# Four graph layers in one kernel: Horner's rule in the last layer, scores beside the context, weights' sums one at a time

## The chip, the cores and the metric

The kernel runs on one core of a Trainium2 chip. The time is the device time of one execution in microseconds (us); all times in this text are microseconds unless marked ns. The core has a matrix engine (TensorE, PE in the rows, with its weight loads as PEld), three engines for elementwise work (VectorE or DVE, ScalarE or ACT, GpSimd or POOL) and a queue that issues most DMAs (SyncE or SP). Everything is float32.

## What is computed

128 graphs of 64 nodes with 512 features pass through four layers. Each layer normalises, applies relu and adds its result to x. Cut to what matters:

```python
h = maximum(layernorm(x), 0)                  # before every layer
# layer 0
agg = adj @ (k * mask); w = D**-0.5 * mask * sum(q * agg, -1)
x += softmax(w over the nodes)[:, None] * (h @ Wv)
# layer 1: q, k, v with biases
W = adj * exp(q @ k.T); x += (W / W.sum(-1)) @ v
# layer 2: 8 heads of 64, q, k, v with biases
P = softmax((q @ k.T) * D_h**-0.5 * (adj + adj)); x += concat(P @ v) @ Wo + bo
# layer 3
e = leaky_relu(sj[None, :] + si[:, None] + ab)
alpha = A * exp(e); Tm = alpha / (alpha.sum(-1) + 1e-12)
x += relu(h @ Wk[0] + Tm @ h @ Wk[1] + Tm @ Tm @ h @ Wk[2] + bk.sum(0))
```

## The kernel before

**Blocks.** The 8192 tokens are 32 blocks of 256 (four graphs), each two tiles of 128 tokens (two graphs). Layers 0 and 1 run for two blocks at a time (layer 0 on b and b+1, layer 1 on b and b+1), then layer 2 for all blocks, then layer 3. x goes through DRAM between layers 1, 2 and 3.

**Products.** A product of a block (256 x 512) with a weight (512 x 512) is done with seven half-size products (the Strassen-Winograd form). `sums` (L203) makes four sums of the activations on POOL (S1, S2, S4, S3; L215 to L218), `formed` (L83) four sums of a weight's quarters (T1, T2, T4, T3). A `Product` (L227) has four accumulators in two PSUM banks, `ab` and `dc`, from a pool of four. `first` issues products 1 and 6 and reads both banks' first state off (`keep_ab`: p1 on ACT, u2 on DVE); `second` issues 5 and 4 and reads p5 off; `late` issues 2, 7 and 3 on top, and `store` adds the pieces up on ACT, DVE and POOL. Product 6 needs S2, product 5 needs S1. `side_by_side` (L339) runs two products with the same activations: first and second of each, then late and store of each, and calls other work (`between`) at three places: after the first's `first`, before the first's `late`, before the second's `late`. A matmul in float32 is two passes of TensorE, so a product is 28 passes of 128x256, or 56 of 128x128 where the output has the features in partitions (`feature_major`, L243).

**Layer 0** multiplies with M, the product of the key and query weights, made once (`folded`, L416: `pf` in the rows, 32 passes), with both weights transposed first (`transpose_weight`, L403: `tw`). At the start the first block's values are multiplied ahead of M (L938 to L942). **Layer 1** has an M of its own, made by `setup1` (L439) inside the first call of `layer1`. Its end takes, per block, the row sums (`den`, L575) and `neighbour_sums` (L377): the matmuls with the attention matrix as weights, 64 rows by 64 columns each, for the four graphs at once in the four quarters of the array.

**Layer 2** per block b: `layer2_scores` (the 64x64 score products into two slots of the PSUM pool `ps_sc`, then softmax), the products for q and k of block b+1, `layer2_turned` (transposes of the softmax), the first half of the values of b+1, `layer2_context` (64x64 products of v and softmax into `ps_sc`, copied out by two ACT copies), the late half of the values, and the output product. Before it, `setup2` (L592) multiplies the values' bias with Wo (`pb`, L608) and adds it to the output bias; that row is added to x on POOL (L991).

**Layer 3** per block: `layer3_norm` (L775: norm, two weighted row sums of h per tile on DVE as `hu` L787, and a diagonal matrix of one of them), then `layer3_in` (L802): a matmul with ones spreads the diagonal (`graph_sums`, L389), e and alpha are made, divided by their row sums and put into a block-diagonal matrix `bd`; two matmuls with `bd` give the transposed transition and its square (`pn`, L833); 16 matmuls multiply h with both (`pz`, L849), ACT copies the result as z, and `sums` is made for h and both parts of z. `layer3_out` (L863) then adds all three products into one pair of accumulators: for each of the seven products, three matmul pairs, one for each Wk. DVE and POOL add the bias, relu and x.

**Order.** Each engine runs its queue in order. The order in the queues comes from the builder: an earlier statement ranks higher, but where an engine would stand idle by the builder's own estimate, ready work of a later statement is put ahead (the trace shows layer 2's loads of adj issued at 21.0). A tile's buffer is reused when its last reader is done.

Of the kernel before, what the change touches and what calls it, by code (L numbers as in the profile page):

```python
# [8 lines left out]
FP = mybir.dt.float32  # L9
AF = mybir.ActivationFunctionType  # L10
ALU = mybir.AluOpType
# [14 lines left out]
def kernel(ctx: ExitStack, tc: tile.TileContext, a: dict, out: bass.AP):  # L26
# [55 lines left out]

    def formed(w, engine):  # L83
        engine.tensor_tensor(w[:, T1], w[:, T3], w[:, B11], ALU.subtract)
        engine.tensor_tensor(w[:, T2], w[:, B22], w[:, T1], ALU.subtract)
        engine.tensor_tensor(w[:, T4], w[:, B21], w[:, T2], ALU.subtract)
        engine.tensor_tensor(w[:, T3], w[:, B22], w[:, T3], ALU.subtract)
# [41 lines left out]
    w0v = fetched("L0_Wv", 1, nc.scalar)  # L129
# [18 lines left out]


    n_bd = 2  # L150
    bds = []
    for i in range(n_bd):
        e = const.tile([P, TT, P], FP, tag=f"bd{i}", name=f"bd{i}")
        nc.gpsimd.memset(e, 0.0)
        bds.append(e)
    turn = [0]

    def next_bd():
        turn[0] += 1
        return bds[turn[0] % n_bd]  # L160
# [61 lines left out]
    class Product:  # L222
# [40 lines left out]
        def first(self, ops, w):  # L263
            self.early(ops, w, (1, 6))
            self.keep_ab()

        def second(self, ops, w, bias=None):
            self.early(ops, w, (5, 4))
            self.keep_dc(bias)
# [69 lines left out]
    def side_by_side(*parts, between=()):  # L339
# [5 lines left out]
        for ops, w, bias, store, name in parts:  # L345
            p = Product(name, bias is not None)
            p.first(ops, w)
            if not made:
                for act in next(between, ()):
                    act()  # L350
            p.second(ops, w, bias)
            made.append(p)
# [77 lines left out]
    def setup0():  # L430
        transpose_weight(f0[1], "k0")
# [7 lines left out]
    def setup1():  # L439


        w1v = fetched("L1_Wv", 3, nc.sync)
        qT, kT = (factor(a[f"L1_W{c}"], c, 1, nc.sync) for c in "qk")
# [28 lines left out]
        return m, u, c, d, w1v, [weight(f"L2_W{c}", 4 + i, nc.sync) for i, c in enumerate("qk")]  # L472


    made1 = []

    def layer0_values(b: int, hT):
        ops = sums(hT, f"0_{b}")
        gv = big.tile([P, 2, TT, D], FP, tag="qk", name=f"gv_{b}")
        return ops, gv, (ops, w0v, None, lambda p: p.store(gv[:, 1]), f"v0_{b}")  # L480

    def layer0(b: int, x, adjT, hs, hT, between, ready=None):

        ops, gv, *part = ready or layer0_values(b, hT)
# [11 lines left out]
        for t, to, at in neighbour_sums(pa, am, hs):  # L496
            nc.scalar.copy(aggs[t][to], pa[t][at])

        side_by_side(
            (ops, m0, None, lambda p: p.store(gv[:, 0]), f"g0_{b}"), *part, between=between  # L500
        )
# [40 lines left out]
    def layer1(b: int, x, adjT, hs, hT, between):  # L542

        if not made1:
            made1.extend(setup1())
# [46 lines left out]
    def setup2():  # L592


        bvc = const.tile([P, K], FP, tag="b2v", name="b2v")
        nc.sync.dma_start(bvc, a["L2_bv"].rearrange("o (k p) -> p (o k)", p=P))
        bo = const.tile([P, D], FP, tag="b2o", name="b2o")
        nc.sync.dma_start(bo, a["L2_bo"].to_broadcast([P, D]))
        wv, wo = fetched("L2_Wv", 0, nc.sync), fetched("L2_Wo", 1, nc.sync)
        yield bo, wv, wo  # L600
        formed(wv, nc.gpsimd)
        yield
        bvr = med.tile([P, K, P], FP, tag="pT", name="bvr2", bufs=3)
        nc.vector.tensor_copy(bvr, bvc.unsqueeze(2).to_broadcast([P, K, P]))
        pb = ps_mm.tile([P, 2, F], FP, tag="mm", name="pb2")
        for j in range(2):
            for k in range(K):
                nc.tensor.matmul(  # L608
                    pb[:, j, :], bvr[:, k, :], wo[:, quarters[k // 2][j], k % 2, :],
                    start=(k == 0), stop=(k == K - 1),  # L610
                )
        nc.vector.tensor_tensor(bo, pb.rearrange("p j f -> p (j f)"), bo, ALU.add)
        formed(wo, nc.gpsimd)
        yield
# [11 lines left out]
    def values(b: int, ops):  # L626

        p = Product(f"v2_{b}")
        p.first(ops, made2[1])
        p.second(ops, made2[1])  # L630
        yield
        p.late(ops, made2[1])
# [455 lines left out]
```

## Time and profile before

| | us |
|---|---|
| median of 3 runs (lowest, highest) | 2751.52 (2751.24, 2751.78) |
| the profiled execution | 2750.76 |
| its span, first to last instruction | 2749.0 |
| first block of layer 0 done (last pass of its M product) | 53.8 |
| layers 0 and 1 on two blocks, a steady period | 61.7 |
| layer 2, a steady block | 28.9 |
| layer 3, a steady block | 22.3 |
| granted TensorE clock, share of full speed | 0.996 |

The page's rows read: line, engine, operation, what it writes <- what it reads (tile names without numbers), shapes, count. Timeline rows begin with the start and the length of a group of like instructions; a bracket at the end gives the idle time before it and what ended it. Matmuls overlap, so their cost is read from one start to the next. Rows of stretches give, for each engine, the busy time.

### The profile page before, as it was taken

What the parts mean: (1) busy time and instruction counts of PE and PEld (TensorE: products, weight loads), DVE (VectorE), ACT (ScalarE), POOL (GpSimd) and SP (SyncE); (2) the same over time, 40 slices, a digit from 0 to 9 for tenths busy, and PEclk for the clock granted to TensorE, in tenths of its full rate; (3) what the DMA queues carried; (4) which work ended last, traced back from release to release, by engine and by line L of the source; (5) the groups of instructions that cost most, each with busy time, mean ns of one, the idle gap of its engine ahead of it and who ended that gap; (6) DMA issues with size and microseconds to landing.
All of it is one profiled execution on the core that took longest, in us unless ns stands there. A gap on an engine that the chain in (4) does not pass through costs nothing.

```text
span 2749.0 us, 53245 instructions
## 1 busy us (share of the span) xinstructions
PE 2696.7 (98%) x21336; PEld 2352.7 (86%) x21336; DVE 1628.3 (59%) x4105; ACT 895.0 (33%) x2132; POOL 1279.6 (47%) x1648
## 2 busy tenths in 40 slices
PE   7899999999999999999999999999989999999999
PEld 5688888888888887899999999999878888888888
DVE  4466666666656667565655655556546555565553
ACT  2233333333333333333333333333322222222221
POOL 2433434343333436555555555554455444444443
PEclk9999999999999999999999999999999999999999
DMA  4111101001111113111111111111111111111110
GB/s 143 40 42 34 49 33 34 34 34 34 44 39 41 41 34 102 38 36 36 53 36 43 46 36 53 36 36 53 48 49 58 57 50 50 50 50 50 50 49 31
DMA packets 102488, 128.53 MB, mean 47 GB/s; under 512 B 40544, under 2 KB 50016, under 8 KB 102240
## 3 DMA queue, kind: packets, MB, share of 16 engines
q1 hardware_dynamic: 100576, 123.02, 13.3%
q8 instruction: 168, 2.75, 0.4%
q10 hardware_dynamic: 1664, 2.10, 0.2%
q14 instruction: 80, 0.66, 0.1%
HBM read 74.76 MB, written 50.33 MB: 46 GB/s over the span
## 4 chain that ended last, share of the span: by engine, by line
PE 87%; DVE 6%; POOL 3%; ACT 2%; DMA 1%; issue 1%; SPq 0%; DVEq 0%; ACTq 0%; POOLq 0%
PE ab_y L250 12%; PE ab_v L250 10%; PE dc_y L250 9%; PE dc_v L250 7%; PE ab_q L243 4%; PE ab_k L243 4%; PE tr L191 4%; PE ab_o L250 4%; PE ab_g L250 4%; PE dc_k L243 3%; PE dc_q L243 3%; PE dc_o L250 3%; PE ab_g L243 3%; PE dc_g L250 2%; PE pz L849 2%; PE dc_g L243 2%
## 5 line engine op out<-in xcount | busy, mean ns | idle before, releaser
L180 ACT ACTIVATE h<-x,nmr,rstd 128x512 f32<-128x512 f32 x256 | 196.5, 807 | 197.8 <-DVE nmr L175 197.6
L173 POOL TENSOR_TENSOR rstd<-ve,neghalf 128x2 f32<-128x2 f32 x128 | 89.4, 699 | 351.3 <-DVE ve L171 351.2
L250 PE MATMUL ab_v<-L_Wv,hT 128*128 128x256 f32 x768 | 200.6, 384 | 2.3 <-DVE u_v L276 1.3
L250 PE MATMUL ab_v<-L_Wv,S 128*128 128x256 f32 x768 | 198.5, 381 | 0.8 <-POOL S L216 0.8
L250 PE MATMUL dc_v<-L_Wv,S 128*128 128x256 f32 x768 | 197.6, 380 | 0.0
L250 PE MATMUL ab_y<-L_Wk,S 128*128 128x256 f32 x768 | 187.3, 380 | 0.0
L168 DVE BATCH_NORM_STATS2 stats<-x 128x6 f32<-128x512 f32 x256 | 165.4, 679 | 27.3 <-DMA x<-x 22.0
L250 PE MATMUL dc_y<-L_Wk,S 128*128 128x256 f32 x768 | 177.9, 381 | 0.0
L194 ACT COPY hT<-tr 128x512 f32<-128x512 f32 x128 | 74.7, 584 | 304.3 <-PE tr L191 280.2
L215 POOL TENSOR_TENSOR S<-hT 128x256 f32<-128x256 f32 x128 | 108.2, 845 | 130.5 <-ACT hT L194 125.0
L250 PEld LDWEIGHTS ab_v<-L_Wv,S 128*128 128x128 f32 x768 | 147.0, 192 | 21.8 <-POOL S L216 1.6
L250 PEld LDWEIGHTS ab_y<-L_Wk,S 128*128 128x128 f32 x768 | 146.5, 191 | 20.1
L250 PEld LDWEIGHTS dc_v<-L_Wv,S 128*128 128x128 f32 x768 | 146.4, 191 | 20.1
L250 PEld LDWEIGHTS dc_y<-L_Wk,S 128*128 128x128 f32 x768 | 143.6, 190 | 18.2
L191 PE MATMUL tr<-ident,h 128*128 128x128 f32 x1024 | 142.5, 280 | 15.5 <-ACT h L180 13.2
L196 DVE COPY hT<-tr 128x512 f32<-128x512 f32 x128 | 87.5, 684 | 110.6 <-PE ab_v L250 106.7
L250 PEld LDWEIGHTS ab_v<-L_Wv,hT 128*128 128x128 f32 x768 | 135.1, 193 | 16.5 <-DVE u_v L276 1.7
L678 POOL TENSOR_TENSOR e<-e,r 128x512 f32<-128x512 f32 x64 | 66.4, 1058 | 163.8 <-DVE r L677 163.8
L191 PEld LDWEIGHTS tr<-ident,h 128*128 128x128 f32 x1024 | 116.2, 142 | 28.9 <-ACT h L180 23.1
L250 PE MATMUL ab_y<-L_Wk,z 128*128 128x256 f32 x512 | 126.3, 379 | 0.0
L787 DVE SCALAR_TENSOR_TENSOR hu<-h,u 128x512 f32<-128x512 f32 x128 | 100.2, 817 | 27.2 <-ACT h L180 27.0
L301 POOL TENSOR_TENSOR gv<-u_g,p_g 128x256 f32<-128x256 f32 x32 | 23.3, 729 | 198.7 <-DVE u_g L298 198.7
(273 smaller groups left out, 6574.8 us busy)
## 6 DMA issues: line engine op xcount, KB each, us to landing
x<-x SPq DMA_DIRECT2D x128, 512.0 KB, 3.4
x<-in_x_dram SPq DMA_DIRECT2D x32, 512.0 KB, 3.6
out_dram<-x SPq DMA_DIRECT2D x31, 512.0 KB, 2.7
adjq<-in_adj_dram SPq DMA_DIRECT2D x64, 64.0 KB, 2.4
L_Wk<-in_L_Wk_dram SPq DMA_DIRECT2D x16, 256.0 KB, 4.2
adjT<-in_adjT_dram SPq DMA_DIRECT2D x32, 64.0 KB, 1.9
L_Wv<-in_L_Wv_dram SPq DMA_DIRECT2D x8, 256.0 KB, 5.3
adj<-in_adj_dram SPq DMA_DIRECT2D x32, 64.0 KB, 2.0
```

What stands on the lines that cost most here:

```text
L168: nc.vector.bn_stats(stats[:, t, :], x[:, t, :])
L173: nc.gpsimd.tensor_tensor(rstd, ve, neghalf, ALU.pow)
L180: nc.scalar.activation(h, x[:, t, :], AF.Relu, bias=nmr[:, t : t + 1], scale=rstd[:, t : t + 1])
L191: nc.tensor.transpose(pt[:, k, :], h[:, k * P : (k + 1) * P], ident)
L194: nc.scalar.copy(ht, pt)
L196: nc.vector.tensor_copy(ht, pt)
L215: nc.gpsimd.tensor_tensor(S1, A21, A22, ALU.add)
L243: nc.tensor.matmul(dst[:, m * P : (m + 1) * P], w[:, place, k, m * P : (m + 1) * P], left[:, k, :], start=key not in self.begun, stop=last ...
L250: nc.tensor.matmul(dst, left[:, k, :], w[:, place, k, :], start=key not in self.begun, stop=last and k == 1, skip_group_check=True,)
L678: nc.gpsimd.tensor_tensor(eh, eh, r.unsqueeze(2).to_broadcast([P, TT * hq, N]), ALU.mult)
L787: nc.vector.scalar_tensor_tensor(hu, hs[t], 1.0, us[s], ALU.mult, ALU.mult, accum_out=sij[:, s, t : t + 1],)
L849: nc.tensor.matmul(pz[t * 2 + g][:, :, c, :], hs[t][h, c * P : (c + 1) * P], tt[h, t], start=True, stop=True,)
```

## The change

Five parts.

1. **Layer 3.** Instead of powers of the transition on h, the products with the weights come first and the transition is applied to the results, twice: h Wk0 + T (h Wk1 + T (h Wk2)). The head multiplies h with Wk2 and Wk1 side by side (y[1] and y[0]); the tail takes the neighbour sum of y[1] with the unnormalised alpha (now built transposed, from adjT), scales it by the reciprocal row sums and adds it to y[0], and multiplies h with Wk0; the end, run within the next block's head, takes the neighbour sum of y[0], scales it on ACT and adds y0, relu and x.
2. **Layer 2.** The scores of block b+1 are issued right behind the context of block b, before the late half of the values, the transposes and the output product. The context goes to the pool `ps_tr` and gets the values' bias when it is copied out, one half on DVE, the other in four ACT steps; `pb` goes.
3. **Weights' sums.** `formed` is split for the weights of layers 2 and 3: `later` puts the four sums on a list, and `chore` issues one on POOL at given places.
4. **Start.** Both weights of layer 0 are transposed and M is made ahead of the first block's products; Wv's loads move from ACT's queue to SP's, its sums from DVE to POOL; of the first block the values come before M's product. `setup1` moves from the start of layer 1 to between blocks 0 and 1 of layer 0.
5. **Side by side.** Where two products run, the order is 1, 5, then 6, 4, and `keep_ab` comes after 6.

```diff
+    def chore(n: int = 1):
+        for _ in range(min(n, len(chores))):
+            w, (to, x, y) = chores.pop(0)
+            nc.gpsimd.tensor_tensor(w[:, to], w[:, x], w[:, y], ALU.subtract)
...
-    w0v = fetched("L0_Wv", 1, nc.scalar)
+    w0v = fetched("L0_Wv", 1, nc.sync)
...
+        def first(self, ops, w, beside: bool = False):
+            self.early(ops, w, (1, 5) if beside else (1, 6))
+            if not beside:
+                self.keep_ab()
+        def second(self, ops, w, bias=None, beside: bool = False):
+            self.early(ops, w, (6, 4) if beside else (5, 4))
+            if beside:
+                self.keep_ab()
             self.keep_dc(bias)
...
     def setup1():
+        qT, kT = (factor(a[f"L1_W{c}"], c, 1, nc.sync) for c in "qk")
         w1v = fetched("L1_Wv", 3, nc.sync)
-        qT, kT = (factor(a[f"L1_W{c}"], c, 1, nc.sync) for c in "qk")
+        yield
...
+        w2 = [fetched(f"L2_W{c}", 4 + i, nc.sync) for i, c in enumerate("qk")]
+        for w in w2:
+            later(w)
...
+        side_by_side(*parts[:: 1 if b else -1], between=between)
...
     def layer2_context(b: int, v, pTs):
-            ps_sc.tile([P, hq, TT, N], FP, tag="sc", name=f"pc_{b}_{g}") for g in range(2)
+            ps_tr.tile([P, hq, TT, N], FP, tag="tr", name=f"pc_{b}_{g}") for g in range(2)
...
-        for g in range(2):
-            nc.scalar.copy(cg[:, :, :, g, :], pcs[g])
+        nc.vector.tensor_tensor(
+            cg[:, :, :, 0, :], pcs[0],
+            bvc.unsqueeze(2).unsqueeze(3).to_broadcast([P, K, TT, N]), ALU.add,
+        )
+        for c in range(K):
+            nc.scalar.activation(
+                cg[:, c, :, 1, :], pcs[1][:, c], AF.Identity, bias=bvc[:, c : c + 1]
+            )
...
     def layer3_in(b: int, x, adjT, hs, e, sj, made: list):
+        pi = graph_sums(e.rearrange("p t i -> p (t i)"), TT * N, f"i_{b}")
...
+        al = small.tile([P, TT, N], FP, tag="am", name=f"al_{b}", bufs=2)
+        nc.vector.tensor_tensor(al, e, adjT, ALU.mult)
         yield
+        made.append((x, al, sums(transposed(hs, f"3_{b}"), f"3_{b}")))
+        yield
+
+    def layer3_head(b: int, ops, between):
+        y = big.tile([P, 2, TT, D], FP, tag="qk", name=f"y12_{b}")
+        side_by_side(*(
+            (ops, w3[i], None, lambda p, i=i: p.store(y[:, i - 1]), f"y{i}_{b}") for i in (2, 1)
+        ), between=between)
+        return y
+
+    def layer3_tail(b: int, al, ops, y):
+        p = Product(f"y0_{b}")
+        p.first(ops, w3[0])
+        p.second(ops, w3[0])
...
+        parts = neighbour_sums(po, al, [y[:, 1, t, :] for t in range(TT)])
...
+        for t, to, at in parts:
+            nc.vector.scalar_tensor_tensor(
+                y[to, 0, t, :], po[t][at], r[at, t : t + 1], y[to, 0, t, :], ALU.mult, ALU.add
+            )
...
+        nc.gpsimd.tensor_tensor(p.u2, p.u2, bs[:, F:], ALU.add)
+        nc.gpsimd.tensor_tensor(p.p5, p.p5, bs[:, F:], ALU.add)
         yield
+        p.late(ops, w3[0])
...
+    def layer3_end(b: int, x, al, y, r, y0):
+        for t, out_at, at in neighbour_sums(po, al, [y[:, 0, t, :] for t in range(TT)]):
+            nc.scalar.activation(tz[t][out_at], po[t][at], AF.Copy, scale=r[at, t : t + 1])
+        for t in range(TT):
+            nc.gpsimd.tensor_tensor(tz[t], tz[t], y0[:, t, :], ALU.add)
...
     prepare(0)
     transpose_weight(f0[0], "q0")
-    formed(w0v, nc.vector)
     turned(0)
-    *ready, part = layer0_values(0, normed[0][1])
-    side_by_side(part)
+    transpose_weight(f0[1], "k0")
     m0, msc = setup0()
+    formed(w0v, nc.gpsimd)
+    loaded[1] = load_x(1, x_d[rows(1), :], 0), load_adjT(1, 0)
+    setup = setup1()
+    next(setup)
     open_end = []
     for i, (layer, b) in enumerate(steps):
-        between = [[], [], []]
+        if i == 1:
+            made1 = next(setup)
+        between = [[], [chore], []]
...
+        y = layer3_head(b, ops, [[begin], [ending.pop()], [lambda: next(stages, None)]])
+        yield
+        tail = layer3_tail(b, al, ops, y)
...
         cT = layer2_context(b, v, pTs)
         part = out_part(b, x, cT)
         if b + 1 < n_blk:
+            es = layer2_scores(b + 1, loaded2[b + 1][1], qk)
+            v = next(coming)
             turned2(b + 2)
-            v = next(coming)
...
         side_by_side(part)
```

`begin` in the head is `layer3_in`'s first part for block b+1 and `layer3_norm` for block b+2; the third place of the head runs `layer3_in`'s second part, the transposes and sums of h of block b+1.

## The prediction

> **What bounds the kernel now.** I read the page's busy shares first, then the stretches by stage, then TensorE's timeline inside one layer-3 block, then the waits.
>
> ```profile
> PE 2696.7 (98%) x21336; PEld 2352.7 (86%) x21336; DVE 1628.3 (59%) x4105; ACT 895.0 (33%) x2132; POOL 1279.6 (47%) x1648
> ```
> ```profile
> 2126.03:2148.33 22.30, 22.30 (x137) 19.73 (x135) 13.11 (x34) 5.75 (x12) 10.90 (x15) 1.00 0.15 51
> 1500.00:1528.92 28.92, 28.92 (x314) 26.78 (x313) 16.54 (x40) 10.14 (x24) 15.69 (x21) 1.00 0.14 42
> ```
>
> The second fence is one block of layer 3 and one of layer 2 (length, then busy time of PE, weight loads, DVE, ACT, POOL). TensorE is busy for the whole stretch, so a steady block changes by what TensorE's own list changes, unless another engine (DVE is next, 13.1 of 22.3) becomes late. TensorE's list in that layer-3 block:
>
> ```profile
> 2122.34 2.75 PE L250 MATMUL dc_y<-L_Wk,S 128*128 128x256 f32 x12
> 2124.93 0.39 PE L392 MATMUL sm_j<-dj,ones_bd 128*128 128x128 f32 x2
> 2125.15 1.04 PE L191 MATMUL tr<-ident,h 128*128 128x128 f32 x8
> 2126.03 1.03 PE L250 MATMUL ab_y<-L_Wk,hT 128*128 128x256 f32 x4
> ...
> 2131.21 0.55 PE L833 MATMUL pn<-eye,bd 128*128 128x64 f32 x4
> 2131.60 2.81 PE L250 MATMUL dc_y<-L_Wk,S 128*128 128x256 f32 x12
> ...
> 2137.38 2.06 PE L849 MATMUL pz<-tt,h 64*128 64x128 f32 x32
> 2139.36 0.92 PE L250 MATMUL ab_y<-L_Wk,hT 128*128 128x256 f32 x3
> ```
>
> Matmuls overlap, so I take start to next start. Each matmul is two passes; a 128x256 pass costs (2124.93 - 2122.34)/12 = 0.216. A block has 84 such passes: 18.13. The graph sum is 0.22, the transposes 0.87, each power of the transition 0.39 (two: 0.78), pz 1.98. Hand-overs between shapes add 0.30, of which pz's entry and exit are 0.19. Sum 22.28, against the measured period of 22.30.
>
> What the changed block will run exists in layer 1 (below), and layer 2's products behind its 64x64 scores show a change of shape (second fence):
>
> ```profile
> 517.39 0.29 PE L575 MATMUL den<-ones_bd,e 64*64 64x1 f32 x8
> 517.53 1.07 PE L384 MATMUL po<-v,e 64*64 64x512 f32 x8
> 518.53 1.13 PE L250 MATMUL ab_g<-fold,hT 128*128 128x256 f32 x4
> ```
> ```profile
> 1509.20 1.16 PE L243 MATMUL ab_q<-hT,L_Wq 128*128 128x128 f32 x8
> 1510.19 1.06 PE L243 MATMUL ab_q<-S,L_Wq 128*128 128x128 f32 x8
> 1511.09 1.06 PE L243 MATMUL dc_q<-S,L_Wq 128*128 128x128 f32 x8
> ```
>
> den is 0.14 and a neighbour sum 1.00. The first eight passes after the scores take 0.99, the next eight 0.90: leaving the 64x64 shape costs 0.10, and entering shows 0.09 in the same way. TensorE's own waits are small and sit at single places (total, times, longest):
>
> ```profile
> PE ab_g L243 <- POOL S L216: 4.3, 15, 0.7
> PE sm_j L392 <- DVE e L661: 3.9, 1, 3.9
> PE ab_q L243 <- POOL S L216: 3.8, 1, 3.8
> ```
>
> **Layer 3 (Horner), 32 blocks.** Removed: both powers (0.78), pz with its hand-overs (1.98 + 0.19), 0.11 of hand-overs round the powers. Added: den 0.14, two neighbour sums 2.00, two visits to the 64x64 shape 0.38. New block: 18.13 + 0.22 + 0.87 + 0.14 + 2.00 + 0.38 = 21.74, that is 0.56 less, times 32 = **-17.8**. [...]
>
> Does anything else become late? By start to start in the same block, DVE loses the row sums, reciprocal and bd (2.1), the 128x512 join (1.3) and five 256-wide steps (0.34 each), 5.1; it gains three u2, six store steps and four y0 steps at 0.34 and three scaled adds (0.76 each in layer 1) with their reciprocals, about 7.1. That makes 15.2 of 21.7. POOL loses eight sums of z and two bias adds (7.5) and gains four 256-wide adds for stores and y0 beside two bias adds (4.4) and two 512-wide adds (2.6): 10.4. ACT stays under 7. [...] hu takes 0.69 alone and 1.21 beside a POOL sum. If every one of the about eight such DVE steps met it, 0.5 each, DVE would be at 19.2, still under 21.7. So I take zero, hidden by TensorE's 18.1 of products; without that cover the most is some 2 us a block. Three new waits, each with cover: y0's first matmul needs y2's banks, read by DVE while y1's late group (2.6) runs; po2 needs y2 stored, with y1's late group and y0's first half (3.5) between; al has two buffers for three blocks, so the next al waits on DVE for po3 of the block before, 8.3 into the step, and behind it in DVE's queue stand y2's store steps, which TensorE wants 6 later.
>
> End: behind the last product now come the last neighbour sum (1.2), the first ACT scaling with its latency (0.8), two POOL adds (1.28 each, over ACT's other scalings), the relu add (0.7) and the store (2.4): 7.7, where 3.6 lies there now: **+4**.
>
> **Layer 2.** Scores move from behind the output product to behind the context: the same 64 passes, one entry (0.09) and part of an exit fewer, 0.16 x 31 = **-5**. Scores issue no DMA. The softmax chain on DVE (six 0.6 steps) now meets the value store and the output's u2; u2 is due 8 us after the scores and what is queued ahead is 7, so zero, at worst 0.5 a block (+15). The bias on the context: one DVE add 0.69 and four ACT steps at about 0.35 instead of two copies at 0.59; the sums of the context start 0.5 later, with 1.3 to spare behind scores, late values and transposes. Bias through Wo: 16 passes, 3.45, go, and the POOL adds of x stop waiting for it (3.8 of wait above, 1.7 of slow passes after it; I take 4.5): **-8**.
>
> **Layer 2 to 3.** Now scores(31) are still unread when layer 3's graph sum needs their PSUM slot (3.9 above, then passes at half pace, 1.5), and later TensorE waits for the same scores' softmax (a wait of 3.1 for POOL's e and what follows it): 12.3 in all (5.8 at the first, 6.5 at the second). With scores a block earlier both waits lose their cause; the context's sums still come short by about 1 and the last weight's four POOL sums may by another 1: **-10**.
>
> **Start.**
>
> ```profile
> 4.20 5.50 ACTq L93 DMA_DIRECT2D L_Wv<-in_L_Wv_dram  x4
> 12.24 0.69 DVE L84 TENSOR_TENSOR L_Wv<-L_Wv 128x512 f32<-128x512 f32 x1 [5.44 <-DMA L_Wv<-in_L_Wv_dram]
> 13.77 1.52 ACT L180 ACTIVATE h<-x,nmr,rstd 128x512 f32<-128x512 f32 x2 [2.70 <-DVE nmr L175]
> ```
>
> ACT issues Wv's loads until 9.7 and DVE stands 5.4 behind Wv's sums, so h comes at 13.8; values then run from 19 to 30, and the timeline has M's first pass (pf) at 33.34. With Wv on SP's queue (behind k; the mask, the biases and x(1) there move back by about 5.5, all due later) and its sums on POOL, k's transposes follow q's at 12 and M starts at 16. M 13.8 plus 1.2 slow, then both products 12.1: the first block is done near 44 instead of 53.8, and two later waits (1.8) fall under the second setup. **-10**; between -4 (k late or slow clock longer) and -13.
>
> **Weights' sums.** Their 1.27 us POOL steps now come with lower rank. But the trace shows that rank is not place: layer 2's value sums, written behind its q and k, ran at 1035.8, two steps early, since POOL was idle. They will again be pulled forward as their loads land. After layer 1's setup 6.9 of stall fall mostly away, because that setup moves one step ahead (its twelve loads on SP wait for M's last pass; x(1), which stood behind them, is now loaded before): **-4.5** (0 to -7). The like stall at 1043 stays: **-1** (0 to -6). Product 5 before 6 avoids the wait for S2 (0.8 in each of 16 pairs), but the next row there, a graph sum, already waits for DVE: **-1** (0 to -13); keeping a and b later costs nothing, as the other product's 3.5 lies before their use.
>
> **Sum.** -17.8 + 4 - 5 - 8 - 10 - 10 - 4.5 - 1 - 1 = -53 from the profiled execution's own 2750.8 (span 2749.0 and 1.8 around it): 2697.5. The median of the runs is 0.8 above it, so 2698.
>
> **Rivals.** (a) Only the steady parts arrive, and the single stalls move to the next wait: -17.8 + 4 - 5 - 3.5 = -22, 2729. For it: stalls here have often a second wait right behind. Chance 0.12. (b) Layer 3 keeps a wait of about 0.5 a block, at po2 or in the two PSUM slots (ps_sc) that graph sum and both neighbour sums now share: 31 x 0.5 = 16 given back, 2714. Chance 0.20. (c) The switch from layer 0 to 1 loses its whole 1.4 in 16 pairs: -22 more, 2676. Chance 0.08. (d) Slower: DVE becomes layer 3's bound. The place is y0's first matmul, which needs the bank that DVE empties in y2's store, behind the norm and four hu steps of the block after next. It decides from 53/31 = 1.7 us a block; DVE's spare of 6.5 must then be gone. At 2.5 a block: 2775. Chance 0.05, since even the pessimistic load above is 19.2. The likeliest case, 0.55, spans 2684 to 2712.
>
> **How the numbers follow.** A measurement of this kernel tells about 0.2% (5.5 us) from no change. Cases (a), (b), (c) and the likeliest lie below 2746, less 0.03 for their edges: faster 0.92, same 0.03, slower 0.05. The range takes the likeliest, (b), half of (a) and half of (c): 2676 to 2729, some 0.84.
>
> **What would show it.** TensorE's instructions fall by 16 x 32 + 16 to 20808; layer 3's period is 21.7 with TensorE busy throughout; M's first pass starts near 16; the graph sum at the start of layer 3 has no wait; the last pass ends 7 to 8 before the span. The forecast is wrong if a layer-3 period is over 22.3, or if TensorE waits in every layer-2 block.

## The result, and the profile after

The changed kernel takes 2734.14 (median of 6 runs, 2730.83 to 2737.18) beside 2751.38 for the kernel before on the same chip (6 runs, 2749.5 to 2751.84): a ratio of 0.9938, 95% interval 0.9925 to 0.9951. It is faster, by 17, where 53 were forecast, and it lies 5 above the top of the range. The profiled execution took 2732.1, its span is 2730.2.

First the busy shares on the page of the changed kernel, with the shares of the chain of waits (the work that ended last, followed back step by step to what released it); the last line is the chain of the kernel before.

```profile
PE 2667.7 (98%) x20808; PEld 2263.4 (83%) x20808; DVE 1704.9 (62%) x4386; ACT 945.8 (35%) x2292; POOL 1291.3 (47%) x1586
...
PE 71%; DVE 17%; POOL 4%; DMA 4%; ACT 2%; issue 2%; SPq 0%; ACTq 0%; POOLq 0%; DVEq 0%
```
```profile
PE 87%; DVE 6%; POOL 3%; ACT 2%; DMA 1%; issue 1%; SPq 0%; DVEq 0%; ACTq 0%; POOLq 0%
```

TensorE's instructions fell to 20808, as forecast. But the chain that ended last now runs through VectorE for 17% of the span, where it was 6%. The work was taken away, and part of what it gave went into waits for VectorE. The stretches of one layer-3 and one layer-2 block (length, then busy time of PE, weight loads, DVE, ACT, POOL) show it:

```profile
2109.90:2131.70 21.80, 21.80 (x119) 17.29 (x118) 14.12 (x41) 6.37 (x15) 10.98 (x13) 1.00 0.15 52
1495.35:1524.46 29.11, 28.91 (x313) 26.75 (x312) 16.79 (x42) 10.25 (x26) 16.14 (x22) 1.00 0.13 43
```

The layer-3 block shown is an undisturbed one, 21.8, with VectorE busy for 14.1 (15.2 was forecast), GpSimd for 11.0 (10.4) and ScalarE for 6.4 (under 7). The layer-2 block is 29.11, where it was 28.92: it has become longer, and TensorE is no longer busy for all of it. TensorE's waits in the whole run (total, times, longest):

```profile
PE sm_w L394 <- DVE wd L511: 9.8, 15, 0.7
PE ab_g L241 <- DVE u_g L278: 7.5, 16, 4.0
PE ab_q L241 <- DVE hT L194: 6.0, 28, 0.4
```

The waits for GpSimd's sums S that stood here before are gone, and so is the one of the first layer-3 graph sum. In their place stand these three waits for VectorE, each in nearly every pair or block of a stage.

Where did the time go? Each stage below runs between the same two passes in both traces; the third column is what the steps of the forecast give for it. The last column is an experiment to which we come at the end.

| stage | before | forecast | changed kernel | last experiment |
|---|---|---|---|---|
| start, to the first steady pair of layers 0 and 1 | 139.1 | -14.5 | -9.5 | -12.6 |
| 14 pairs of layers 0 and 1 and one block of layer 0 | 879.2 | -1 | 0.0 | +0.4 |
| turn to layer 2, to its first output product | 110.3 | -9 | -2.7 | -12.4 |
| 28 blocks of layer 2 | 809.7 | -4.5 | +7.2 | -6.9 |
| turn to layer 3, five blocks of it, and the end | 208.5 | -9 | -4.6 | -7.4 |
| 27 blocks of layer 3 | 602.2 | -15 | -9.2 | -14.0 |
| span | 2749.0 | -53 | -18.8 | -52.9 |

(In the changed kernel the turn to layer 2 contains one set of scores more, 1.1, and the turn to layer 3 one less. The last experiment's column is its profiled execution, 2698.1, the fastest of four.) The first block's M begins at 19.6, not near 16, since a transpose waits 3.3 for a copy on VectorE, and the last pass ends 7.7 before the span, as forecast. Layers 0 and 1 keep their 61.7. Of the 34 that are missing against the forecast, 11.7 are in layer 2, 6.3 in the turn to it, 5.8 in layer 3, 5.0 in the start and 4.4 in the turn to layer 3. Three places follow: the weights' sums, layer 2's block, and layer 3's.

**The weights' sums, at 1028** (the timeline; a bracket gives the idle time and what ended it):

```profile
1028.12 3.71 POOL L98 TENSOR_TENSOR L_Wv<-L_Wv 128x512 f32<-128x512 f32 x3
...
1030.66 3.39 DVE L538 SCALAR_TENSOR_TENSOR x<-gv,att,x 128x512 f32<-128x512 f32 x2
1031.79 5.83 POOL L98 TENSOR_TENSOR L_Wo<-L_Wo 128x512 f32<-128x512 f32 x4
...
1033.97 1.27 DVE L166 BATCH_NORM_STATS2 stats<-x 128x6 f32<-128x512 f32 x2
...
1035.24 0.39 DVE L278 TENSOR_TENSOR u_g<-ab_g,p_g 128x256 f32<-128x256 f32 x1
...
1035.68 2.08 PE L241 MATMUL ab_g<-hT,fold 128*128 128x128 f32 x8 [4.00 <-DVE u_g L278]
```

All eight sums of two weights run one behind the other as soon as their loads have landed, although most of them are written at later places. Beside them two VectorE steps take 3.39; the same two steps take 1.41 in an earlier pair with no sum beside them (first line below). Behind these two in VectorE's queue stand the norm and u_g, and TensorE waits 4.00; its next passes then run at a granted clock of 0.53 for 3.4. A like row of eight stands at 80 to 91, behind layer 1's setup. But this stall is not new. The kernel before has it too (second line), and TensorE waits 4.08 there; the forecast let it stand but for 1.

```profile
890.22 1.41 DVE L538 SCALAR_TENSOR_TENSOR x<-gv,att,x 128x512 f32<-128x512 f32 x2
```
```profile
1040.74 3.40 DVE L538 SCALAR_TENSOR_TENSOR x<-gv,att,x 128x512 f32<-128x512 f32 x2
```

New in the turn to layer 2 are five waits for VectorE further on, 1.68, 1.77, 1.54, 1.68 and 0.89, together 7.6 (before, two waits for ScalarE stood there, 0.7 and 1.1).

**Layer 2, behind the context** (timeline):

```profile
1517.43 0.69 DVE L703 TENSOR_TENSOR cT<-pc,b2v 128x512 f32<-128x512 f32 x1 [0.43 <-PE pc L695]
...
1518.35 1.29 DVE L644 TENSOR_TENSOR e<-s,adjq 128x512 f32<-128x512 f32 x2 [0.23 <-PE s L634]
...
1520.74 1.81 DVE L654 TENSOR_TENSOR e<-e,mx 128x512 f32<-128x512 f32 x2
...
1521.00 1.04 PE L189 MATMUL tr<-ident,h 128*128 128x128 f32 x8
...
1522.81 1.26 DVE L659 TENSOR_REDUCE r<-e 128x8 f32<-128x512 f32 x2
...
1524.85 0.68 DVE L194 COPY hT<-tr 128x512 f32<-128x512 f32 x1
```

The transposes of the next h are done at 1522.0, but VectorE has its half of the context, the softmax chain and the value store in front of the copy and gets to it at 1524.85. Before, it stood idle for 3.2 ahead of the same copy:

```profile
1529.32 0.69 DVE L196 COPY hT<-tr 128x512 f32<-128x512 f32 x1 [3.16 <-PE ab_v L250]
```

TensorE wants the copy for the next q product.

**Layer 3, at y1's first product** (timeline):

```profile
2088.13 0.69 DVE L776 SCALAR_TENSOR_TENSOR hu<-h,u 128x512 f32<-128x512 f32 x1
...
2088.75 0.42 DVE L846 TENSOR_TENSOR y<-ab_y,bs 128x256 f32<-128x256 f32 x1
...
2089.09 0.41 DVE L847 TENSOR_TENSOR u_y<-ab_y,p_y 128x256 f32<-128x256 f32 x1
2089.42 0.68 DVE L776 SCALAR_TENSOR_TENSOR hu<-h,u 128x512 f32<-128x512 f32 x1
2089.55 1.13 PE L248 MATMUL ab_y<-L_Wk,hT 128*128 128x256 f32 x4
```

y1 takes the banks of the y0 before it, which L846 and L847 empty. One of layer 3's weighted row sums (hu) has been put ahead of them, and another ahead of the two steps that empty the second bank. The four passes at 2089.55 take 1.27 from start to start instead of 0.86. It isn't so in every block: the mean period is 21.96, the undisturbed one 21.78.

### The profile page after: what moved, and what is told of

It reads as the page before. It is cut to its first block, busy times and chain, and to the rows that moved or that the text cites. A ratio compares the mean times of both kernels' runs of the same rounds, so it can differ in the third digit from the quotient of the medians.

```text
span 2730.2 us, 52850 instructions
## 1 busy us (share of the span) xinstructions
PE 2667.7 (98%) x20808; PEld 2263.4 (83%) x20808; DVE 1704.9 (62%) x4386; ACT 945.8 (35%) x2292; POOL 1291.3 (47%) x1586
## 4 chain that ended last, share of the span: by engine, by line
PE 71%; DVE 17%; POOL 4%; DMA 4%; ACT 2%; issue 2%; SPq 0%; ACTq 0%; POOLq 0%; DVEq 0%
PE ab_y L248 10%; PE dc_y L248 8%; PE ab_v L248 7%; PE dc_v L248 6%; PE ab_q L241 4%; PE ab_g L248 4%; PE ab_k L241 4%; PE ab_g L241 3%; PE po L386 3%; PE dc_k L241 3%; PE dc_q L241 3%; PE dc_g L248 2%; PE tr L189 2%; DMA x<-x 2%; PE dc_g L241 2%; DVE e L654 2%
## 5 line engine op out<-in xcount | busy, mean ns | idle before, releaser
L248 PE MATMUL ab_y<-L_Wk,hT 128*128 128x256 f32 x768 | 204.3, 388 | 3.3 <-DVE u_y L300 2.6
L248 PE MATMUL dc_y<-L_Wk,S 128*128 128x256 f32 x768 | 199.8, 383 | 0.7
L248 PE MATMUL ab_y<-L_Wk,S 128*128 128x256 f32 x768 | 197.8, 380 | 0.0
L248 PEld LDWEIGHTS ab_y<-L_Wk,hT 128*128 128x128 f32 x768 | 137.8, 190 | 70.1 <-issue 25.2
L248 PEld LDWEIGHTS dc_v<-L_Wv,S 128*128 128x128 f32 x768 | 145.8, 190 | 21.9 <-DVE v L302 2.1
L862 POOL TENSOR_TENSOR tz<-tz,y 128x512 f32<-128x512 f32 x64 | 92.9, 1452 | 145.8 <-ACT tz L860 145.8
L323 POOL TENSOR_TENSOR qk<-u_q,p_q 128x256 f32<-128x256 f32 x32 | 23.3, 727 | 265.4 <-DVE u_q L307 265.4
L189 PE MATMUL tr<-ident,h 128*128 128x128 f32 x1024 | 135.8, 275 | 3.9 <-ACT h L178 2.2
L278 DVE TENSOR_TENSOR u_v<-ab_v,p_v 128x256 f32<-128x256 f32 x96 | 40.6, 423 | 126.2 <-ACT p_v L277 126.2
L213 POOL TENSOR_TENSOR S<-hT 128x256 f32<-128x256 f32 x128 | 99.4, 776 | 35.5 <-ACT hT L192 33.1
L216 POOL TENSOR_TENSOR S<-hT 128x256 f32<-128x256 f32 x128 | 106.9, 835 | 1.6 <-DVE hT L194 0.4
```

The lines of the kernel that those rows point to most:

```text
L189: nc.tensor.transpose(pt[:, k, :], h[:, k * P : (k + 1) * P], ident)
L213: nc.gpsimd.tensor_tensor(S1, A21, A22, ALU.add)
L216: nc.gpsimd.tensor_tensor(S3, A11, A21, ALU.subtract)
L248: nc.tensor.matmul(dst, left[:, k, :], w[:, place, k, :], start=key not in self.begun, stop=last and k == 1, skip_group_check=True,)
L278: nc.vector.tensor_tensor(self.u2, self.b, self.p1, ALU.add)
L862: nc.gpsimd.tensor_tensor(tz[t], tz[t], y0[:, t, :], ALU.add)
```

## The experiments

Each run is compared with runs of the kernel before on the same chip; the changed kernel's ratio, 0.9938, is what the ratios are held against. The combinations, and the ordered copies of h, change several things; the others change one.

**Scores behind the output product again.**

```diff
             cT = ... # context
-            es = layer2_scores(b + 1, loaded2[b + 1][1], qk)
             v = next(coming)
...
         side_by_side(part)
+        es = layer2_scores(b + 1, loaded2[b + 1][1], qk)
```

> The changed kernel with one thing undone: layer 2's scores stand behind the output product again; the context keeps its bias steps and its place in PSUM. Theory 1 (VectorE's queue): with scores beside the context, VectorE has its half of the context, the six softmax steps, the value store and the copy of the transposed h back to back, so the copy comes late and TensorE waits 0.35 in every block. Undone, that wait goes and the block takes 28.9 instead of 29.1. Against it layer 3's first graph sum waits again for scores still unread (5 to 6). Together 2730 to 2735. Rival (the context's bias steps, or its place in PSUM, make the block longer): the block stays at 29.1 and the time is 2737 or more.

2724.16, ratio 0.9906 (0.9893 to 0.9920): faster than both theories had it. The block takes 28.97 (median) and the wait for the copy is gone, as theory 1 says; the bias steps alone cost next to nothing (28.92 before). What theory 1 had wrong is the second half: layer 3's first graph sum does not wait either way. So it was not the scores' earlier place that took that wait away. What is left is the context's move to another PSUM pool, which leaves a slot for the graph sum; no run moves the context back alone.

**Both copies of the transposed h on ScalarE.**

```diff
-            if t % 2:
+            if both or t % 2:          # both: in layer 2
                 nc.scalar.copy(ht, pt)
```

> The changed kernel with both copies of layer 2's transposed h on ScalarE, where one was on VectorE. Theory 1: TensorE's wait for that copy goes, and so do the two passes of the next q product that are pulled ahead and change the shape once more; a layer-2 block takes 28.7 to 28.8, 0.35 less than now, so 10 less in 29 blocks: 2724. Rival (another step is due just behind: the output's u2 on VectorE or the sums of h on GpSimd): the wait gets another name and the block stays at 29.0 to 29.1, 2733.

2758.32, ratio 1.0027 (1.0017 to 1.0036): 24 slower than the changed kernel. Neither theory. The wait for the copy is gone; the longest of TensorE's waits is now

```profile
PE pc L695 <- ACT pT L678: 20.9, 56, 0.8
```

With one more step on ScalarE the builder put the norm's two ScalarE steps of the block after next ahead of the copies of the transposed softmax; these stood ready while ScalarE waited for the norm, and the context waits for them twice in every block (the next run shows that it is this order). The repair of one queue had changed the order of another.

**The same, with that order held.** The norm's ScalarE steps are tied, in issue order only, behind the softmax copies:

```diff
-            prepare2(b + 2)
+            with tc.issue_after(turned_out[0]):
+                prepare2(b + 2)
```

> As the run with both copies of layer 2's transposed h on ScalarE, but with the norm's two ScalarE steps tied behind the copies of the transposed softmax, which they overtook there (the context waited 0.4 twice in each block). Theory 1: with that wait gone too, TensorE runs through, and a layer-2 block takes 28.7 to 28.8: 2723. Rival (layer 2 has no cover left on ScalarE or VectorE, and the wait shows up at a third place): 29.0 or more, 2732 or more.

2726.57, ratio 0.9914 (0.9900 to 0.9928). Theory 1 for the block: this stretch is one block,

```profile
1519.60:1548.30 28.70, 28.70 (x314) 26.72 (x313) 15.89 (x42) 10.65 (x27) 16.16 (x21) 1.00 0.13 43
```

28.7 with TensorE busy throughout, 0.22 less than before the change. But every fourth or fifth block takes 1.5 more, and so the run gains 7.5 and not 11: there x lands late, and VectorE stands at it ahead of the step that empties the q product's bank (a new wait, ab_v for DVE's stats, 6.8 in all).

**Weights' sums where they are written.** Each is tied behind the GpSimd instruction written ahead of it:

```diff
-            nc.gpsimd.tensor_tensor(w[:, to], w[:, x], w[:, y], ALU.subtract)
+            tc.keep_in_program_order(
+                nc.gpsimd.tensor_tensor(w[:, to], w[:, x], w[:, y], ALU.subtract)
+            )
```

> The changed kernel with each of the weights' sums tied behind the GpSimd instruction that is written ahead of it, so that it runs where it is written and is not pulled forward. Theory 1 (contention): at 85 and at 1031 two VectorE steps of 512 wide take 3.4 together beside GpSimd's weight sums, and the norm's power on GpSimd stands behind four sums, so TensorE waits 2.0, 2.3 and 1.7 there, and 4.2 and 1.6 at 1031. Spread out, most of it goes: 8 to 10 less, 2725. Rival (those waits belong to the first step of layer 1 and to the turn from layer 1 to 2 whatever GpSimd does): 2732 to 2735.

2735.20, ratio 0.9939 (0.9926 to 0.9953): no change. The rival's number, but not its reason. The wait of 4.0 at 1031 is gone, and the turn to layer 2 is 4.9 shorter. In exchange one pair of layers 0 and 1 takes 2.3 more, and the first five blocks of layer 2 take 30.7, 34.4, 30.7, 30.9 and 29.3 instead of 29.1. At their written places the sums cost TensorE as much as they did where the builder had put them.

**No sums at all.**

```diff
     def later(w, name):
-        chores.extend((w, s) for s in sums_of_weights)
+        for to in (T1, T2, T4):
+            nc.sync.dma_start(w[:, to], a[name][:F, :F].rearrange("(k p) o -> p k o", p=P))
```

> The changed kernel without the twenty sums of layer 2's and layer 3's weights; their places are filled by plain loads of a quarter, so this leaves out a part of the computation. Theory 1 (each 512-wide sum on GpSimd holds up VectorE steps beside it, wherever it is put): the waits at 85 to 95, at 1031, and part of those at 1049, 1073 and 1091 go, 12 to 16 less: 2720. Rival (only the row of eight at 1031 costs anything): 4 to 6 less, 2729. Second rival (the waits come from the turns themselves): 2733.

2719.00, ratio 0.9884 (0.9871 to 0.9898). Theory 1: 15 less. The start is 4.8 shorter, and the turn to layer 2 is 7.2 shorter than in the changed kernel; that makes -14.3 and -9.9 against the kernel before, where -14.5 and -9 were forecast. But the turn gets there by another path than the forecast had: the stall at 1028, which was to stay, is gone, and three of the new waits (1.66, 2.40 and 0.34) are still there. (The sums are 28, not twenty as the expectation counts them: four for each of seven weights. The loads that fill the places move 5.5 MB more.)

**Sums on VectorE.**

```diff
-            nc.gpsimd.tensor_tensor(w[:, to], w[:, x], w[:, y], ALU.subtract)
+            nc.vector.tensor_tensor(w[:, to], w[:, x], w[:, y], ALU.subtract)
```

> The changed kernel with the weights' sums of layers 2 and 3 on VectorE instead of GpSimd, nothing else. Theory 1 (the two engines' steps hold each other up; alone a sum costs VectorE 0.69): the waits at 85 and at 1031 shrink to about half: 2724. Rival (in the run that did this among other repairs the gain of 10 came from the order of VectorE's queue that it brought along): 2731 or more.

2721.12, ratio 0.9892 (0.9879 to 0.9906). Theory 1, and more than half: nearly all that leaving the sums out gains. So the cost is not the adds: 28 sums on the busier engine (0.69 each, by the sum of Wv at 12.24 in the kernel before) cost TensorE about 2 (less than these ratios can tell apart), and on the idler one 15. Two things go at once: no sums run on GpSimd beside VectorE's steps (beside them the changed kernel's two steps took 3.39 and not 1.41), and GpSimd's part of the norm no longer stands behind them (in the changed kernel its input was ready at 1036.42 and it began at 1037.58). How the 13 divide between the two was not taken apart.

**Layer 3's row sums behind the store steps.**

```diff
+                with tc.issue_after(stored[0]) if stored else ExitStack():
                     nc.vector.scalar_tensor_tensor(hu, hs[t], 1.0, us[s], ...)
```

(`stored` holds the last VectorE step of the y0 before.)

> The changed kernel with layer 3's four weighted row sums tied behind the store steps of the block before on VectorE. Theory 1: TensorE's small wait at the second product of the head comes because one of these row sums (0.7) is put ahead of the two steps that empty that product's bank; without it the period of layer 3 falls from 21.96 to 21.8, 4 less: 2730. Rival (the wait is set by the output's PSUM, the neighbour sums or ScalarE): the period stays, or grows because the spread diagonal comes later.

2725.89, ratio 0.9913 (0.9899 to 0.9926). Theory 1: from the fourth on every period is 21.8 (21.78 in the mean), and TensorE has no wait in them. The rest of the gain of 8 lies within what the runs of the changed kernel differ by among themselves.

**Layer 1's row sums behind the spread weights**, in the same way, to take the wait of 0.7 in 15 pairs.

```diff
+            with tc.issue_after(spread[0]):
                 nc.vector.scalar_tensor_tensor(hc, hs[t], 1.0, c1, ...)
```

(`spread` holds the step that makes wd in the layer-0 block before.)

> The changed kernel with layer 1's weighted row sums (hc) tied behind the spread softmax weights (wd) of layer 0 on VectorE; in the trace one hc step of 1.2 is put ahead of wd, and TensorE waits 0.7 for wd in 15 of 16 pairs. Theory 1: wd comes 1.2 earlier, the wait goes, a pair of blocks in layers 0 and 1 takes 60.9 to 61.0 instead of 61.7, 10 to 12 less in all: 2723. Rival (the passes behind the graph sum wait for VectorE or for GpSimd's sums S just as long, as the wait for S did before the change): the period stays at 61.7, 2733.

2733.27, ratio 0.9939 (0.9927 to 0.9952). The rival. wd comes earlier and its wait is gone, and in its place stands

```profile
PE ab_g L241 <- DVE u_g L278: 18.4, 15, 3.9
```

The period is 61.6 instead of 61.7. In this stretch TensorE waits for VectorE in both orders of its queue.

**The old order of products side by side.**

```diff
-            p.first(ops, w, len(parts) > 1)
+            p.first(ops, w)
...
-            p.second(ops, w, bias, len(parts) > 1)
+            p.second(ops, w, bias)
```

> The changed kernel with part five undone: where two products run side by side the order is 1, 6, then 5, 4 again, and both first states are read off as before. Theory 1 (VectorE sets the pace of the stretch from layer 0 to layer 1, by the row sums, the spread weights and the first products' u2 one behind the other): the order of the products doesn't matter there, the pair stays at 61.7, and the time stays within 3 of 2734. Rival (product 5 ahead of 6 saved a wait for S2 that comes back): 0.8 in 16 pairs and a little in layer 2, 13 more: 2747.

2724.39, ratio 0.9903 (0.9888 to 0.9917). The pair stays at 61.7, as theory 1 has it, and the wait for S is back (4.4 in 15). Neither theory expected the gain of 10: the turn to layer 2 is 3.5 shorter, the turn to layer 3 1.8, and the 27 blocks of layer 3 3.7.

**The same in layer 3 alone.**

```diff
-            p.first(ops, w, len(parts) > 1)
+            p.first(ops, w, beside and len(parts) > 1)   # beside=False from layer 3's head
```

(and `second` likewise.)

> The changed kernel with part five undone in layer 3 alone: its two products side by side go 1, 6, then 5, 4 again; layers 0 to 2 keep 1, 5, then 6, 4. Theory 1: with 5 ahead of 6 the head wants the second bank of the product before it 0.86 earlier, while VectorE is still emptying it behind a weighted row sum; undone, layer 3's period is 21.8 throughout, 5 less in 27 blocks, and nothing else moves: 2728 to 2729. Rival (the whole gain of 10 of the run with the old order everywhere comes from the turns, and layer 3's period fell there by chance of the queue's order): 2733.

2731.69, ratio 0.9926 (0.9912 to 0.9939): too near to tell from the changed kernel by its time. The trace has most of what theory 1 says for layer 3: 3.7 less in the 27 blocks, where 5 were expected. "Nothing else moves" failed, though every engine's order is the same up to layer 3: the turn to layer 2 took 3.1 more. Here are the stretches behind the same two waits, this run first; the third number from the end is the clock that TensorE was granted, as a share of full speed:

```profile
1094.00:1102.00 8.00, 6.62 (x33) 6.43 (x34) 3.24 (x10) 1.93 (x6) 2.77 (x3) 0.61 0.01 3
```

and the changed kernel:

```profile
1093.50:1101.00 7.50, 6.57 (x56) 6.38 (x57) 3.22 (x9) 2.29 (x8) 2.84 (x4) 1.00 0.01 3
```

Behind waits of 1.7 and 0.9 the one execution went on at a granted clock of 0.61, the other at full clock. One thing ahead of them does differ: a wait 8 earlier took 1.8 in the first and 1.5 in the second.

**Combinations.** The first has both row-sum edits and the scores behind the output product.

> The changed kernel with three edits together: layer 3's weighted row sums behind the store steps, layer 1's behind the spread weights, and layer 2's scores behind the output product. Theory 1 (three separate waits): the gains add up, 8 + 10 + 10 less than 2734: 2706. Rival (the second edit brings nothing, since another wait stands behind it): 2716.

2718.27, ratio 0.9886 (0.9871 to 0.9901). The rival, in line with the run of layer 1's row sums alone.

The second has layer 3's row sums and the ordered copies of h.

> The changed kernel with two repairs: layer 3's weighted row sums behind the store steps, and both copies of layer 2's transposed h on ScalarE with the norm's steps behind the copies of the softmax; scores stay beside the context. Theory 1: the two gains add up, 8 + 7.5 less than 2734: 2718. Rival (they share a wait at the turn from layer 2 to 3): 2722 or more.

2722.82, ratio 0.9899 (0.9882 to 0.9915). The rival's number, but the traces don't show its reason: the span is 10.9 shorter than the changed kernel's, where the two repairs alone give 5.8 and 6.2. The 8 and 7.5 of the expectation came from medians. Both steady periods are there (28.7 and 21.8), and so are the blocks of layer 2 with a late x.

The third adds a fifth buffer for x:

```diff
-        x = big.tile([P, TT, D], FP, tag="x", name=f"x{stage}_{b}", bufs=4)
+        x = big.tile([P, TT, D], FP, tag="x", name=f"x{stage}_{b}", bufs=5)
```

> As the run before, with five buffers for x instead of four. In the run with the ordered copies every fifth block of layer 2 took 1.5 more, because x came 1.5 late (its load waits for the store that frees the buffer) and VectorE stood at it ahead of the step that empties the q product's bank. Theory 1: with a spare buffer these go, 6 times 1.5: 2709. Rival (the load is late for another reason, its place in the queue or the memory): no change, 2718.

2722.97, ratio 0.9896 (0.9881 to 0.9911). The late blocks are still there. The buffer came, but the builder put the load and VectorE's first steps on x a block earlier with it, so VectorE stood as close behind the load as before.

The fourth adds the weights' sums on VectorE:

> As the run before, with the weights' sums of layers 2 and 3 on VectorE, where a 512-wide step takes 0.69, instead of GpSimd, where it takes 1.27 and holds up VectorE's steps beside it. Theory 1 (it is the two engines' steps holding each other up that costs): the waits at 85, 1031 and 1073 shrink, 5 to 8 less than the run before. Rival (VectorE is what those stretches wait for, so any step more on it costs the same): within 3 of the run before, or more.

2713.00, ratio 0.9862 (0.9847 to 0.9876). Theory 1, and more: 10 less, where 5 to 8 were expected.

The fifth adds the old order of products and goes back to four buffers:

> The changed kernel with four repairs: weighted row sums of layer 3 behind the store steps, both transposed copies of layer 2 on ScalarE with the norm behind the softmax copies, weights' sums on VectorE, and the old order of products side by side; four buffers for x. Theory 1: against the run of 2713 only the turn from layer 1 to 2 gains, 3.5: 2709. Rival (with the old order the pair of layers 0 and 1 waits for S2 more often once the sums are gone): 2713 or more.

2715.65, ratio 0.9871 (0.9857 to 0.9884). The rival: with VectorE relieved, the old order brings nothing more, and the wait for S costs 5.5 in 16.

The sixth has five buffers again, and VectorE's norm steps tied behind the k product's u2:

```diff
+            with tc.issue_after(turned_out[0]), tc.issue_after(last_u2[0]):
                 prepare2(b + 2)
```

> As the run before, with five buffers for x and VectorE's norm steps of layer 2 tied behind the k product's u2, so that they are not pulled a block ahead as soon as the buffer is there. Theory 1: x is there when VectorE comes to it, and the 1.5 in every fifth block of layer 2 goes: 10 less than the run before, 2699. Rival (VectorE, held back, is late with the q product's store and the wait spreads over all blocks): 2709 or more.

2700.78, ratio 0.9818 (0.9805 to 0.9832), 15 less than the fifth. Theory 1, but only in part: of the 14.1 between the two traces 6.4 lie in the 28 blocks of layer 2, the rest in the turns to layers 2 and 3, of which the expectation says nothing. The third combination showed that the fifth buffer alone brings nothing; the tie alone was not run. Its busy shares, its chain and one block each of layers 3 and 2:

```profile
PE 2657.1 (99%) x20808; PEld 2262.8 (84%) x20808; DVE 1694.0 (63%) x4382; ACT 961.8 (36%) x2324; POOL 1268.7 (47%) x1558
...
PE 86%; DVE 7%; POOL 3%; ACT 2%; issue 1%; DMA 1%; ACTq 0%; POOLq 0%; SPq 0%; DVEq 0%
```
```profile
2058.30:2080.10 21.80, 21.80 (x120) 17.39 (x119) 15.17 (x42) 7.38 (x16) 11.14 (x13) 1.00 0.16 52
1496.90:1525.60 28.70, 28.70 (x314) 26.70 (x312) 16.71 (x40) 10.82 (x27) 16.13 (x21) 1.00 0.14 43
```

Every one of its 28 layer-2 periods is 28.7, and from the fourth on every layer-3 period is 21.8 or 21.9. VectorE's share of the chain is back at 7%. It is the fastest kernel of this study, 1.8% ahead of the kernel before and some 33 ahead of the changed one, and TensorE runs the same number of passes as in the changed kernel.

## Why the forecast was wrong, step by step

The forecast took a list of TensorE's passes and added next to nothing for the other engines. The list was right where a block runs undisturbed: 21.78 in layer 3, where 21.74 was forecast, and 28.70 in layer 2, where 28.92 less 0.16 was. What failed is the value zero, or nearly so, for what VectorE and GpSimd would do to it.

The last column of the table, -52.9 in all where the forecast's sum was -53, supports this less than it seems. That kernel undoes part five, has its sums on VectorE and a fifth buffer. Its profiled execution is the fastest of four; by the medians it gains 49. And its granted clock is 0.999 where it was 0.996 before; 0.003 of 2696 is 8 (an estimate from these two clocks), of which the forecast's slow passes, 1.7 and 1.5 (clocks of 0.52 for 3.5 and 0.54 for 3.2 in the kernel before), make up 3. So the near equality is partly luck.

- **Layer 3, -17.8.** The passes were right: 21.74 forecast, 21.78 with no wait. The step that failed is "So I take zero": 27 blocks gained 9.2 and not 15. The wait was foreseen as rival (b) but at the wrong place, at po2 or the PSUM slots. It stands at y1's banks, behind the row sums in VectorE's queue; VectorE had 7.7 of 21.8 free. It was a matter of order, not of load: tied behind the store, the row sums cost nothing, with VectorE busy for 15.3 of the block. Part five had a share in it, since it calls for the second bank 0.86 earlier: with the old order in layer 3 alone the wait nearly goes as well (21.83 in the mean).
- **Layer 2, -5.** The failing step is "u2 is due 8 us after the scores and what is queued ahead is 7, so zero". The stage took 7.2 more. The forecast named the right queue and the price "at worst 0.5 a block"; measured are 0.35 of wait (start to start) and 0.12 for the passes of q pulled ahead, less what the scores save. It looked at u2, though, and not at the copy of the transposed h, which is due earlier, and it counted the chain's third step at 0.6 each where it took 0.9 beside GpSimd's sums. So the move as it was made is a loss: undone, the run is 10 faster. Without that wait it saves 0.22 a block (0.16 was forecast).
- **Bias through Wo, -8.** The passes went, 3.45, and so did the wait of 3.8 behind the bias row with its slow passes (a clock of 0.52 for 3.5). The step that failed is one that was put at nothing without a reason: no wait was to take its place. Five did, 7.6 in all, each for VectorE, and the turn gave 2.7 instead of 9. That it gives 9.9 with the sums left out is luck: a stall goes that the forecast let stand, and 4.4 of the new waits stay.
- **Weights' sums, -4.5 - 1.** What failed is "6.9 of stall fall mostly away": behind layer 1's setup TensorE still waits 1.8 and 2.2, and 3.5 at a granted clock of 0.51 behind the second cost 1.7 more (an estimate: 3.5 times 0.49), 5.7 in all. The text before the result said that the sums would be pulled forward as their loads land, and that rank is not place, and then credited the setup all the same. Here the same should have been weighed that the forecast weighed for layer 3, a VectorE step beside a GpSimd sum: two steps of 1.41 together become 3.39 beside the sums.
- **Product 5 before 6, -1.** The wait for S went and the wait for wd took its place: 0. The failing step is that the order "costs nothing": undone everywhere, the run is 10 faster. The forecast looked for a cost in keeping a and b, and only in layers 0 and 1; it left out that the order calls for the second bank earlier in the products side by side of layer 3. There that is 3.7 of the 10; how the rest, in the turns, comes from the order was not taken apart.
- **Start, -10.** The sum came out, its parts did not. The first block is done at 47.8, 6 earlier and not 10, because M began 3.6 later than forecast. With the sums left out the start as a whole is 14.3 shorter, where -10 and -4.5 were forecast together: what came behind the first block gave more than it was credited with. That the two make up for each other is luck.
- **Layer 2 to 3, -10, and end, +4.** The end was right (+4.1). The first wait lost its cause, but not by the scores' place, as the run with the scores put back shows. Of the -4.4 that are missing in this stage, 2.6 are one wait in the second block of layer 3. There y0's first matmul waits for the bank that y2's store empties, behind four row sums: the very place of rival (d), at one block instead of all.
- **Rivals.** Most of the shortfall is waits that moved on to the next queue, which rival (a) had for the single stalls alone (0.12) and (b) for layer 3 alone (0.20). They happened together, and the range held no case for that: the cases were treated as alternatives, though most hang on one thing, VectorE's order. That the gain would not be less than 22 was the thing to doubt.

What stays open: the pair of layers 0 and 1, where TensorE still waits about 0.7 to 0.9 for VectorE in each of 16 pairs; no run here takes this wait away without another in its place.

## What to carry to other kernels

When an edit moves work onto an engine that is only 60% busy, look at what is in its queue between the moved step and the next thing that TensorE waits for, and cost that stretch alone; the mean share, 62% here, did not show it. After an edit, read which engine the chain of waits runs through: a share that went from 6% to 17% with TensorE still at 98% busy tells that the gain is waiting behind that engine's order. And where a builder orders the queues by its own estimate, tie the few steps that must not overtake; here three such ties, with the sums and a copy on other engines, a fifth buffer and the old order of products, were worth about twice the change itself (33 against 17).

## What the runs showed of the hardware that was not expected

- Passes behind short waits can cost as much as the waits. Behind waits of 1.7 and 0.9 TensorE went on at a granted clock of 0.61 for 8 in one execution (the old order in layer 3 alone), which is 3 in a span (an estimate: 8 times 0.39), and at 1.00 in another (the changed kernel). In the changed kernel the clock was 0.53 for 3.4 behind a wait of 4.0 and 0.51 for 3.5 behind one of 2.2, but 1.00 behind one of 1.8 (at 88.32). What decides it was not shown.
- A 512-wide sum takes 1.27 on GpSimd (median) and 0.69 on VectorE (the sum at 12.24 in the kernel before), but VectorE's steps beside it on GpSimd are drawn out too (two of 1.41 together became 3.39): 28 of them made 15 on TensorE's path, against about 2 when VectorE did them itself.
